# Layer norm of a vision-Mamba kernel: statistics on 64 partitions, the mean subtracted by VectorE, a product on GpSimd

## The chip, the core and the metric

The kernel runs on one core of one Trainium2 chip. The metric is the device time of an execution in microseconds (us). Three runs of the kernel before gave 31715.66, 31737.26 and 31752.72 us; the median is 31737.26 us.

## The reference, cut to what matters

Eight images of 64 x 64 pixels with 96 channels go through four Mamba layers one after the other. Each layer normalizes its input, projects it to 192 inner channels, filters these with a small convolution, runs a selective scan over the pixels (in four directions in layers 0 to 2, in one in layer 3) and comes back to 96 channels. Between the scan and the way back, layers 0 to 2 have a layer norm over the 192 inner channels of each pixel, and then the gate. In layer 0 it reads:

```python
mu = y.mean(-1, keepdims=True)
var = y.var(-1, keepdims=True)
y = (y - mu) * jax.lax.rsqrt(var + 1e-05) * ln_gamma + ln_beta
y = y * jax.nn.silu(z)
return y @ out_proj_w.T
```

Layers 1 and 2 compute the same; layer 3 has the gate and the projection without the norm. All is fp32.

## The kernel before, in words

One hardware loop (L145) runs over the 8 images; its body holds the four layers. Channels lie on partitions and the 4096 pixels of an image along the free axis, in chunks of 512 pixels (CH). The 192 inner channels are more than the 128 partitions, so every inner tensor has two parts: channels 0 to 127 (the tile y_a), and channels 128 to 191, which take 64 partitions (the tile y_b; after the scan its two 64-partition halves each hold a partial sum, which have still to be added).

A layer's scan takes most of its time. The order of its work is written out by hand, slot by slot (the table "plan", L935), and is the same before and after the change. What comes after the scan, from L509 on, is not written out by hand: there the framework decides the order of the instructions on each engine, and each engine then works through its own queue in that order. The framework also sets the semaphores between the engines. One semaphore counter stands for each engine, and a step of it may stand for several instructions.

The stage after the scan has two parts.

*The norm*, L516 to L543, works on a pair of chunks at a time, four pairs a layer. TensorE computes everything that sums over channels, by multiplying with constant matrices:

- "ca" (L524, L525): y_a less its mean, for each of the two chunks. The matrix cen_a is the identity less 1/192, and neg is -1/192 everywhere. A tile of 128 partitions and two banks of PSUM ("wide", two buffers, which the scan uses for "dbu").
- "cb" (L528): y_b less the mean, the two halves of y_b added at the same time. The two chunks stand one above the other in one bank, 64 partitions each ("mm", two buffers).
- The squares of both (L530, L534) are made by ScalarE, and TensorE sums them up to the variance "var" on 128 partitions (L535 from sq_a, L537 from sq_b), in a bank for each chunk (the function "single", the banks y0 and y1, which have one buffer each).
- ScalarE makes 1/sqrt(var + eps) out of it as exp(-0.5 ln(...)) (L540 Ln, L541 Exp). VectorE multiplies ca by it into y_a (L542) and cb into y_b (L543, 64 partitions a chunk).

*The gate stage*, L546 to L596, also works on pairs. GpSimd scales the layer's input (L553, tile "xc", in the pool "decays" with six buffers). TensorE multiplies it by weights (L556 "z_a", one matmul for each chunk in a "wide" tile; L559 "z_b", both chunks in one "mm" bank). ScalarE applies SiLU (L572). VectorE scales the normalized y by gamma and adds beta (L574) and multiplies it by the gate (L582). TensorE projects back to 96 channels (L587, L589, in the banks y0 and y1). VectorE adds the result to the layer's input (L593), takes the statistics for the next layer's normalization (L214), and SyncE writes it to memory (L596). The scan's last additions to y_a and y_b stand in L932, before all this.

A matmul in fp32 shows in the profile as two records. Where a matmul has 64 output columns, two of them, on different columns of the array, can stand side by side.

Of the kernel before, what the change touches and what calls it, by code (L numbers as in the profile page):

```python
# [22 lines left out]
F32 = mybir.dt.float32  # L23
AF = mybir.ActivationFunctionType
ALU = mybir.AluOpType
# [5 lines left out]
DI = 192  # L31
# [4 lines left out]
CH = 512  # L36
# [3 lines left out]


SEL, IDENT, GROUPS, MEAN = 0, 64, 192, 288
NEGMEAN, CEN_A, CEN_B, ONE, EPS, N_CONST = 416, 544, 672, 736, 737, 738


class Layer:
# [61 lines left out]
@contextmanager  # L108
def tables(tc, name):

    load = tc.keep_in_program_order(tc.nc.scalar.preload_act_table_set(name))
    with tc.issue_after(load.ins):
        yield
# [3 lines left out]
def kernel(ctx: ExitStack, tc: tile.TileContext, x_in, const_in, *rest):  # L117
# [27 lines left out]
    with tc.For_i(0, x_in.shape[0], 1) as b:  # L145

        of = x_in[bass.ds(b, 1)].rearrange("o c l -> (o c) l")
        x = load_x(tc, env, of)
        for n, ly in enumerate(LAYERS):
            if n == len(LAYERS) - 1:  # L150
                to = x_out[bass.ds(b, 1)].rearrange("o c l -> (o c) l")
            else:
                to = env.dram.tile([C, L], F32, tag="x", name=f"x_mem{n}")
            x = layer(tc, env, x, of, to, n, ly)
            of = to
# [9 lines left out]
def layer(tc, env, x, x_of, x_to, n, ly):  # L165

    nc = tc.nc
    const, small, big = env.const, env.small, env.big
    sel = const[:, SEL : SEL + 64]
    ident = const[:, IDENT : IDENT + 128]  # L170
    mean_w = const[:, MEAN : MEAN + 128]
    R, K = ly.rank, ly.dirs
    XP = 33 + R

    def mm(name):
        return env.ps_m.tile([128, CH], F32, tag="mm", name=name)

    def wide(name):

        return env.ps_b.tile([128, 2 * CH], F32, tag="dbu", name=name)  # L180
# [4 lines left out]
    def piece(name):  # L185
        return env.deltas.tile([128, CH], F32, tag="delta", name=name)
# [37 lines left out]
    mean = small.tile([C, 1], F32, name="mean")  # L224
# [3 lines left out]
    var = small.tile([C, 1], F32, name="var")  # L228
# [3 lines left out]
    scale = small.tile([C, 1], F32, name="scale")  # L232
# [28 lines left out]
    halves = [slice(0, 64), slice(64, 128)]  # L261
    widths = ((0, 128), (128, 64))

    def single(o, name):
        return env.ps_y.tile([128, CH], F32, tag=f"y{o}", name=name)
# [10 lines left out]
    def u_chunk(half, c):  # L276
        return u0[half][c // 4][0 : widths[half][1], c % 4 * CH : c % 4 * CH + CH]
# [79 lines left out]
    def make_ys():  # L357
        return [big.tile([128, L], F32, tag=f"big{o}", name=f"y{o}") for o in range(2)]

    work = scans(  # L360
        tc, env, n, ly, w, u_mem, lambda half: u_chunk(half, 0), d, neg_a, make_ys, mm, wide
    )
# [145 lines left out]
    y_a, y_b = ys  # L508
# [6 lines left out]
    chunks = [slice(c * CH, (c + 1) * CH) for c in range(NCH)]  # L515
    if ly.norm:  # L516
        with tables(tc, "natural_log_exp_and_others"):
            neg, cen_a = const[:, NEGMEAN : NEGMEAN + 128], const[:, CEN_A : CEN_A + 128]
            cen_b = const[:, CEN_B : CEN_B + 64]
            for c in range(0, NCH, 2):  # L520
                pair = chunks[c : c + 2]
                ca, cb = wide("ca").rearrange("p (o l) -> p o l", o=2), mm("cb")
                for o, s in enumerate(pair):
                    nc.tensor.matmul(ca[:, o], cen_a, y_a[:, s], start=True, stop=False)  # L524
                    nc.tensor.matmul(ca[:, o], neg, y_b[:, s], start=False, stop=True)  # L525
                for first, weights, y in ((True, neg[:, 0:64], y_a), (False, cen_b, y_b)):
                    for s, at in zip(pair, halves):
                        nc.tensor.matmul(cb[at], weights, y[:, s], start=first, stop=not first)  # L528
                sq_b = piece("sq_b")
                nc.scalar.activation(sq_b, cb, AF.Square)  # L530
                var = [single(o, "var") for o in range(2)]
                for o in range(2):
                    sq_a = piece("sq_a")
                    nc.scalar.activation(sq_a, ca[:, o], AF.Square)  # L534
                    nc.tensor.matmul(var[o], mean_w, sq_a, start=True, stop=False)  # L535
                for o, at in enumerate(halves):
                    nc.tensor.matmul(var[o], mean_w[at], sq_b[at], start=False, stop=True)  # L537
                for o, (s, at) in enumerate(zip(pair, halves)):
                    rstd = piece("rstd")
                    nc.scalar.activation(rstd, var[o], AF.Ln, bias=const[:, EPS : EPS + 1])  # L540
                    nc.scalar.activation(rstd, rstd, AF.Exp, scale=-0.5)  # L541
                    nc.vector.tensor_tensor(y_a[:, s], ca[:, o], rstd, ALU.mult)  # L542
                    nc.vector.tensor_tensor(y_b[at, pair[0]], cb[at], rstd[at], ALU.mult)  # L543


    with tables(tc, "silu_and_others"):  # L546
        for c in range(0, NCH, 2):
            pair = chunks[c : c + 2]
            z_a, z_b = wide("z_a").rearrange("p (o l) -> p o l", o=2), mm("z_b")
            xcs = []  # L550
            for o in range(2):
# [3 lines left out]
                at = ly.win_z  # L555
# [29 lines left out]
            at = ly.w_out  # L585
# [8 lines left out]
            if c % 4 == 2:  # L594
                half = slice(c // 4 * L // 2, (c // 4 + 1) * L // 2)
# [445 lines left out]
def constants():  # L1041
    a = np.zeros((128, N_CONST), np.float32)
    for p in range(128):
        a[p, SEL + p % 64] = 1
        a[p, IDENT + p] = 1
    a[32, ONE] = a[96, ONE] = 1
    for p in range(C):
        g = GROUPS + p // GROUP * GROUP
        a[p, g : g + GROUP] = 1 / GROUP
    a[:, MEAN : MEAN + 128] = 1 / DI  # L1050
    a[:, NEGMEAN : NEGMEAN + 128] = -1 / DI
    a[:, CEN_A : CEN_A + 128] = np.eye(128) - 1 / DI
    a[:, CEN_B : CEN_B + 64] = np.tile(np.eye(64), (2, 1)) - 1 / DI
    a[:, EPS] = 1e-5
    return a
# [52 lines left out]
def layouts(inputs):  # L1108
    arrays = {"x": inputs["x"].reshape(-1, L, C).transpose(0, 2, 1), "const": constants()}
    for n, (ly, (pre, names)) in enumerate(zip(LAYERS, _NAMES)):  # L1110
        arrays[f"pack{n}"] = pack(
            ly, inputs[pre + "conv_w"], *(inputs[pre + s] for s in names.split())
        )
    for n, (ly, (pre, _)) in enumerate(zip(LAYERS, _NAMES)):
        arrays[f"conv{n}"] = inputs[pre + "conv_w"].reshape(DI, ly.taps).T.reshape(-1)
    return {f"in_{k}_dram": np.ascontiguousarray(v) for k, v in arrays.items()}
# [20 lines left out]
```

## Time and profile before

| what | value |
|---|---|
| median of the runs | 31737.26 us |
| the profiled execution | 31703.4 us |
| its span on the core | 31698.6 us |
| granted TensorE clock over the span | 0.98 |
| from the last L932 to the first gate (L572), layer 0, image 0 | 38.80 us: TensorE busy 36.32, VectorE 14.75, ScalarE 17.68, GpSimd 3.28, clock 0.99 |
| from there to the end of the layer | 27.42 us: TensorE busy 23.17, VectorE 19.32, ScalarE 7.80, GpSimd 1.17, clock 0.87 |

How to read the lines: a group of instructions has the source line, the engine, the operation, what is written and read, the shape, the count, and behind the bar the busy time in us and the mean of one in ns; behind the second bar stands the engine's idle time before them and what ended it ("<-PE var L537": ScalarE had waited for TensorE's var of line 537). In a timeline the first number is the start in us, the second the duration of the (merged) instructions, and the bracket holds the idle time before. PEld is the loading of weights. In a table of stretches every engine has its busy us and, in brackets, its instructions; the last three figures are the granted clock of TensorE, the DMA share and GB/s. TensorE, VectorE, ScalarE and GpSimd are PE, DVE, ACT and POOL.

### The profile page before, as it was taken

The numbers are of one execution on the slowest core, as the hardware profiler recorded it, in microseconds if no ns is written. First come the engines' busy times: TensorE is split into PE (matmuls) and PEld (weight loads), VectorE is DVE, ScalarE is ACT, GpSimd is POOL, SyncE is SP. The second block draws the span as 40 slices with busy tenths as digits, with TensorE's granted clock in tenths as the row PEclk, the third lists the DMA queues.
The fourth block names the chain that finished last, engine by engine and source line by source line (L and its number), as shares of the span: only waits on it lengthen the run. The fifth ranks groups of instructions, "written<-read, shape, count | busy, mean of one in ns | idle before, by whom it ended". The sixth has DMA issues, their size and how long they took to land. (4 is left out here: it accounts for less than half of the span.)

```text
span 31698.6 us, 951914 instructions
## 1 busy us (share of the span) xinstructions
PE 30814.0 (97%) x402320; PEld 16776.3 (53%) x402320; DVE 28392.2 (90%) x29432; ACT 26085.1 (82%) x65064; POOL 27178.5 (86%) x9436
## 2 busy tenths in 40 slices
PE   9999999999999999999999999999999999999999
PEld 5555555555555545555455554555555555555555
DVE  9899898998989989899898998989989899898998
ACT  8788788887888878888788887878878888788887
POOL 8898788987889879898798987989878898788987
PEclk9999999999999999999999999999999999999999
DMA  3333233333333333333333333333323333333332
GB/s 90 78 76 85 72 90 79 75 86 73 89 80 74 87 72 88 80 74 87 73 88 80 74 87 74 87 79 74 87 72 89 80 74 86 72 90 79 75 86 72
DMA packets 1262156, 2544.89 MB, mean 80 GB/s; under 512 B 108560, under 2 KB 129296, under 8 KB 1234832
## 3 DMA queue, kind: packets, MB, share of 16 engines
q1 hardware_dynamic: 1257872, 2483.64, 33.3%
q8 instruction: 3192, 52.30, 0.7%
q14 instruction: 1092, 8.95, 0.1%
HBM read 2208.74 MB, written 274.46 MB: 78 GB/s over the span
## 5 line engine op out<-in xcount | busy, mean ns | idle before, releaser
L890 POOL TENSOR_TENSOR h<-h,c 128x2048 f32<-128x2048 f32 x4992 | 22723.0, 4557 | 1867.5 <-ACT state L886 625.9
L872 DVE TENSOR_TENSOR_SCAN h<-d_a,state,dbu 128x512 f32<-128x512 f32 x17472 | 21076.5, 1261 | 1130.2 <-PE dbu L841 687.9
L858 ACT ACTIVATE d_a<-delta,neg_a 128x512 f32<-128x512 f32 x19968 | 14166.5, 716 | 122.1 <-DVE h L872 101.3
L841 PE MATMUL dbu<-diag,du_t 64*64 64x128 f32 x319488 | 11142.2, 277 | 296.4 <-DVE h L872 224.7
L841 PEld LDWEIGHTS dbu<-diag,du_t 64*64 64x64 f32 x319488 | 8712.0, 133 | 5111.5 <-issue 4681.5
L904 PE MATMUL y_ps<-h,const 128*64 128x512 f32 x39936 | 10827.0, 617 | 119.1 <-POOL h L890 110.5
L786 ACT ACTIVATE diag<-const,bt 128x64 f32<-128x64 f32 x25600 | 7550.4, 344 | 14.0 <-PE dbu L841 7.8
L773 POOL TENSOR_TENSOR diag<-const,bt 128x512 f32<-128x512 f32 x3328 | 3475.2, 1045 | 335.0 <-ACT bt L747 246.3
L872 DVE TENSOR_TENSOR_SCAN h<-d_a,dbu 128x512 f32<-128x512 f32 x2496 | 2881.8, 1203 | 498.6 <-ACT d_a L858 216.2
L904 PEld LDWEIGHTS y_ps<-h,const 128*64 128x64 f32 x39936 | 2065.6, 135 | 1899.4 <-issue 1498.5
L716 PE MATMUL v<-w,x_dbl 39*128 39x208 f32 (+1 forms) x6656 | 2618.4, 477 | 8.3 <-DVE delta_t L752 7.3
L716 PEld LDWEIGHTS v<-w,x_dbl 39*128 39x128 f32 (+1 forms) x6656 | 1787.2, 317 | 1568.3 <-issue 883.1
L824 ACT COPY delta<-delta_ps 64x512 f32<-64x512 f32 x3328 | 1930.9, 580 | 566.7 <-PE delta_ps L815 519.6
L815 PEld LDWEIGHTS delta_ps<-const,delta_t 128*64 128x64 f32 (+1 forms) x19968 | 1637.0, 154 | 1415.7 <-issue 949.7
L815 PE MATMUL delta_ps<-const,delta_t 128*64 128x128 f32 (+1 forms) x19968 | 2223.8, 286 | 11.6 <-issue 11.6
L747 ACT COPY bt<-v 128x32 f32<-128x32 f32 x1664 | 300.8, 183 | 1848.7 <-PE v L716 1846.5
L730 PEld LDWEIGHTS u_t<-const,u 128*128 128x128 f32 x3328 | 650.1, 195 | 1583.2 <-issue 887.2
L886 ACT COPY state<-h 128x4 f32<-128x4 f32 x4992 | 972.4, 195 | 568.0 <-DVE h L872 527.9
L454 POOL TENSOR_TENSOR acc<-acc,more 128x512 f32<-128x512 f32 x576 | 756.7, 1317 | 699.6 <-ACT more L453 356.1
L730 PE MATMUL u_t<-const,u 128*128 128x128 f32 x3328 | 1292.2, 388 | 0.0
L320 PE MATMUL conv<-xn,taps 96*128 96x512 f32 (+1 forms) x2496 | 1160.0, 658 | 22.1 <-DVE taps L203 22.1
L731 PE MATMUL u_t<-const,u 64*128 64x64 f32 x3328 | 1098.8, 330 | 0.0
(99 smaller groups left out, 16194.5 us busy)
## 6 DMA issues: line engine op xcount, KB each, us to landing
c<-cm SPq DMA_DIRECT2D x1792, 512.0 KB
c<-xm SPq DMA_DIRECT2D x1536, 512.0 KB
u<-u SPq DMA_DIRECT2D x1088, 256.0 KB
u<-u SPq DMA_DIRECT2D x1088, 128.0 KB
u<-u SPq DMA_DIRECT2D x48, 1024.0 KB
x_mem<-x SPq DMA_DIRECT2D x48, 768.0 KB
x<-x_mem SPq DMA_DIRECT2D x48, 768.0 KB
x<-in_x_dram SPq DMA_DIRECT2D x32, 768.0 KB
```

Of the source, the lines that this page charges most:

```text
L320: nc.tensor.matmul(part, taps[:, t, d0 : d0 + nd], rhs, start=t == 0, stop=t == ly.taps - 1)
L716: nc.tensor.matmul(turned[i, e, "v"][:, b], block(2 * e + b, dbls[i]), w[0:XP, at : at + DI + NS], start=True, stop=True,)
L730: nc.tensor.transpose(to[:, b, 0:128], block(b_, u_of(i, 0)), ident)
L773: nc.gpsimd.tensor_tensor(diags[i, 0][:, b], sel.unsqueeze(1).unsqueeze(3).to_broadcast([128, NH, 64, 2]), of.unsqueeze(2).to_broadcast([1 ...
L786: nc.scalar.activation(diags[i, 1][:, b, q // 2, :, q % 2], sel, AF.Copy, scale=turned[i, b // 2, "b"][:, b % 2, NJ + q : NJ + q + 1],)
L815: nc.tensor.matmul(block(b, to), of_, ident, start=True, stop=True)
L824: nc.scalar.copy(delta[64 * half : 64 * half + 64], of)
L841: nc.tensor.matmul(to[64 * half : 64 * half + 64, e, b], du[rows, b, 64 * t : 64 * t + 64], diag[rows, b, 2 * half + pair], start=True, st ...
L858: nc.scalar.activation(d_a, deltas[i, t], AF.Exp, scale=neg_a[:, at : at + 1])
L872: nc.vector.tensor_tensor_scan(hs[s][:, m4, flow], decays.pop(m)[:, flow], p[:, flow], 0.0 if first else states[i // NCH][:, j : j + 1], A ...
L890: nc.gpsimd.tensor_tensor(hs[s], hs[s], cs[i, g], ALU.mult)
L904: nc.tensor.matmul(sums[i][o][64 * half : 64 * half + 64], sel, hs[of][:, state, :], start=g == 0 and e in (0, 4), stop=g == 1 and e in (3 ...
```

## The change

The norm stage is written anew; all else stays.

- The mean of the pair is computed by itself, on 64 partitions a chunk, with the two chunks side by side in one bank ("mean", bank y0). "ca" and its constant cen_a are gone.
- VectorE subtracts the mean from y_a in place. As the mean stands on 64 partitions, it takes two instructions of 64 partitions for each chunk.
- "cb" is computed as before. The square of y_a is taken from SBUF.
- "var" is on 64 partitions a chunk too, both chunks in one bank (bank y1). One Ln serves both. The Exp spreads the result to 128 partitions, with two instructions of 64 partitions for each chunk. The tiles ln and rstd come from the pool "decays" that xc uses, three a pair.
- GpSimd multiplies y_a by it; VectorE multiplies cb into y_b as before.
- The table of constants shrinks from 738 to 482 columns.

```diff
-NEGMEAN, CEN_A, CEN_B, ONE, EPS, N_CONST = 416, 544, 672, 736, 737, 738
+NEGMEAN, CEN_B, ONE, EPS, N_CONST = 352, 416, 480, 481, 482
...
-            neg, cen_a = const[:, NEGMEAN : NEGMEAN + 128], const[:, CEN_A : CEN_A + 128]
-            cen_b = const[:, CEN_B : CEN_B + 64]
+            neg, cen_b = const[:, NEGMEAN : NEGMEAN + 64], const[:, CEN_B : CEN_B + 64]
+            mean_w = const[:, MEAN : MEAN + 64]
             for c in range(0, NCH, 2):
-                pair = chunks[c : c + 2]
-                ca, cb = wide("ca").rearrange("p (o l) -> p o l", o=2), mm("cb")
-                for o, s in enumerate(pair):
-                    nc.tensor.matmul(ca[:, o], cen_a, y_a[:, s], start=True, stop=False)
-                    nc.tensor.matmul(ca[:, o], neg, y_b[:, s], start=False, stop=True)
-                for first, weights, y in ((True, neg[:, 0:64], y_a), (False, cen_b, y_b)):
-                    for s, at in zip(pair, halves):
-                        nc.tensor.matmul(cb[at], weights, y[:, s], start=first, stop=not first)
+                pair = list(zip(chunks[c : c + 2], halves))
+
+                mean, cb = single(0, "mean"), mm("cb")
+                for p, work in (
+                    (mean, ((mean_w, y_a), (mean_w, y_b))),
+                    (cb, ((neg, y_a), (cen_b, y_b))),
+                ):
+                    for last, (weights, y) in enumerate(work):
+                        for s, at in pair:
+                            nc.tensor.matmul(
+                                p[at], weights, y[:, s], start=not last, stop=bool(last)
+                            )
+                var = single(1, "var")
+                for s, at in pair:
+                    for half in halves:
+                        nc.vector.tensor_tensor(
+                            y_a[half, s], y_a[half, s], mean[at], ALU.subtract
+                        )
+                    sq_a = piece("sq_a")
+                    nc.scalar.activation(sq_a, y_a[:, s], AF.Square)
+                    nc.tensor.matmul(var[at], mean_w, sq_a, start=True, stop=False)
                 sq_b = piece("sq_b")
                 nc.scalar.activation(sq_b, cb, AF.Square)
-                var = [single(o, "var") for o in range(2)]
-                for o in range(2):
-                    sq_a = piece("sq_a")
-                    nc.scalar.activation(sq_a, ca[:, o], AF.Square)
-                    nc.tensor.matmul(var[o], mean_w, sq_a, start=True, stop=False)
-                for o, at in enumerate(halves):
-                    nc.tensor.matmul(var[o], mean_w[at], sq_b[at], start=False, stop=True)
-                for o, (s, at) in enumerate(zip(pair, halves)):
-                    rstd = piece("rstd")
-                    nc.scalar.activation(rstd, var[o], AF.Ln, bias=const[:, EPS : EPS + 1])
-                    nc.scalar.activation(rstd, rstd, AF.Exp, scale=-0.5)
-                    nc.vector.tensor_tensor(y_a[:, s], ca[:, o], rstd, ALU.mult)
-                    nc.vector.tensor_tensor(y_b[at, pair[0]], cb[at], rstd[at], ALU.mult)
+                for s, at in pair:
+                    nc.tensor.matmul(var[at], mean_w[at], sq_b[at], start=False, stop=True)
+                ln = env.decays.tile([128, CH], F32, tag="d_a", name="ln")
+                nc.scalar.activation(ln, var, AF.Ln, bias=const[:, EPS : EPS + 1])
+                for s, at in pair:
+                    rstd = env.decays.tile([128, CH], F32, tag="d_a", name="rstd")
+                    for half in halves:
+                        nc.scalar.activation(rstd[half], ln[at], AF.Exp, scale=-0.5)
+                    nc.gpsimd.tensor_tensor(y_a[:, s], y_a[:, s], rstd, ALU.mult)
+                    nc.vector.tensor_tensor(y_b[at, pair[0][0]], cb[at], rstd[at], ALU.mult)
```

The order that the framework gives the changed program: on TensorE, the first of a pair's mean matmuls stands ahead of the previous pair's last var matmuls, the other three behind them. On VectorE, the four subtractions of a pair are mixed with the two y_b products of the pair before (subtraction, product, subtraction, product, subtraction, subtraction), and the three gamma scalings of the pair before follow. On GpSimd, six of the eight products of a layer stand ahead of the first xc, the seventh behind it, then the second xc, the eighth product and the other six xc. In the gate stage z_a and z_b of all pairs stand behind the norm's last matmul; before, the z_a of pair 0 stood ahead of it.

More of the change, by code (lines that the diff above doesn't have):

```diff
@@ L170, in layer @@
     ident = const[:, IDENT : IDENT + 128]
-    mean_w = const[:, MEAN : MEAN + 128]
     R, K = ly.rank, ly.dirs
@@ L1049, in constants @@
         a[p, g : g + GROUP] = 1 / GROUP
-    a[:, MEAN : MEAN + 128] = 1 / DI
-    a[:, NEGMEAN : NEGMEAN + 128] = -1 / DI
-    a[:, CEN_A : CEN_A + 128] = np.eye(128) - 1 / DI
+    a[:, MEAN : MEAN + 64] = 1 / DI
+    a[:, NEGMEAN : NEGMEAN + 64] = -1 / DI
     a[:, CEN_B : CEN_B + 64] = np.tile(np.eye(64), (2, 1)) - 1 / DI
```

## The prediction

> **What bounds the kernel now.** I read the page first, then the groups by line, then the timeline of one layer norm. On the page TensorE (PE) is busy all the time, in every slice.
>
> ```profile
> span 31698.6 us, 951914 instructions
> PE 30814.0 (97%) x402320; PEld 16776.3 (53%) x402320; DVE 28392.2 (90%) x29432; ACT 26085.1 (82%) x65064; POOL 27178.5 (86%) x9436
> ```
>
> A busy share of the whole says little about one stage, so I went to the norm's groups. Three layers with a norm in each of 8 images make 24 norm stages of four pairs of chunks, 96 pairs.
>
> ```profile
> L524 PE MATMUL ca<-y,const 128*128 128x512 f32 x384 | 213.6, 638 | 0.0
> L535 PE MATMUL var<-sq_a,const 128*128 128x512 f32 x384 | 180.5, 592 | 0.0
> L540 ACT ACTIVATE rstd<-var,const 128x512 f32<-128x512 f32 x192 | 130.4, 679 | 297.7 <-PE var L537 297.7
> L542 DVE TENSOR_TENSOR y<-ca,rstd 128x512 f32<-128x512 f32 x192 | 132.8, 691 | 579.7 <-ACT rstd L541 579.7
> L543 DVE TENSOR_TENSOR y<-cb,rstd 64x512 f32<-64x512 f32 x192 | 131.3, 684 | 3.0
> ```
>
> PE waits for nothing there (idle 0.0), ScalarE (ACT) waits for PE, VectorE (DVE) for ACT: PE sets the pace. The timeline of the stage that begins at 1138 us gives the period of a pair:
>
> ```profile
> 1150.85 1.12 PE L524 MATMUL ca<-y,const 128*128 128x512 f32 x2
> 1152.77 1.94 PE L528 MATMUL cb<-y,const 128*64 128x512 f32 x8
> 1154.63 1.12 PE L524 MATMUL ca<-y,const 128*128 128x512 f32 x2
> 1156.45 1.88 PE L535 MATMUL var<-sq_a,const 128*128 128x512 f32 x4
> 1158.27 1.13 PE L537 MATMUL var<-sq_b,const 64*128 64x512 f32 x4
> 1159.32 1.12 PE L524 MATMUL ca<-y,const 128*128 128x512 f32 x2
> ...
> 1177.52 1.52 POOL L553 TENSOR_SCALAR xc<-x,scale,shift 96x512 f32<-96x512 f32 x2 [34.29 <-PE z_b L559]
> 1178.36 0.67 DVE L543 TENSOR_TENSOR y<-cb,rstd 64x512 f32<-64x512 f32 x1
> 1178.99 0.69 DVE L542 TENSOR_TENSOR y<-ca,rstd 128x512 f32<-128x512 f32 x1
> 1179.71 0.69 DVE L543 TENSOR_TENSOR y<-cb,rstd 64x512 f32<-64x512 f32 x1
> 1179.83 3.75 PE L556 MATMUL z_a<-xc,w 96*128 96x512 f32 x4 [2.48 <-DVE y L542]
> ```
>
> From start to start: 1.92 (ca of one chunk) + 1.86 (cb, four matmuls in two columns of the array) + 1.82 (ca) + 1.82 (var) + 1.05 (var from sq_b) = 8.47 us. At the end PE stands still for 2.48 us, and the same two matmuls then take 3.75 us instead of 2. The stretches show why:
>
> ```profile
> 1180.00:1182.00 2.00, 2.00 (x3) 0.97 (x4) 1.97 (x4) 1.83 (x4) 0.00 (x0) 0.50 0.00 0
> 1188.00:1190.00 2.00, 2.00 (x7) 0.57 (x4) 2.00 (x4) 0.60 (x1) 0.00 (x0) 1.00 0.00 0
> ```
>
> The granted clock (third figure from the end) was 0.50 after the gap and 1.00 later.
>
> **What the Trainium skill says.** "TensorE: Matmul & The Clock Gate", Part 1: an idle window of some 3.4 us halves the clock until a busy one has passed. The trace agrees and is stricter: a 2.48 us gap was enough here. "TensorEngine Tiling (Array Packing)", Key Properties: tiles work side by side, a change of tiling mode drains the array. The trace agrees: eight cb records took 1.94 us, as four of var did (1.88). "VectorE: DVE Perf Modes", Two Vector instructions with no wait between them: an instruction whose inputs or output start in another quadrant of partitions is held until the one before has finished. The trace agrees: from L543 on the low half to L542 it is 0.63 us from start to start, from L542 to L543 on the upper half 0.72. "GPSIMD Engine Reference", 3.1: an addition of two fp32 tensors of 2048 takes 4497 ns; L890 shows 4557. The same page, 8, says that GpSimd blocks VectorE only where the latter has two SBUF inputs or a two-port mode; the new subtractions have one input in PSUM, so I add nothing. No run here shows it for this pair of operations.
>
> **The change part by part.** Times t count from the end of the last addition to y_b (1141.47 in the stage above). Durations: an fp32 matmul is two passes 0.43 apart, 0.86, its result 0.16 later; DVE 0.69; Square 0.60, Ln 0.69, Exp 0.63, starting 0.52 apart (two L534 took 1.08 in all, so neighbours overlap by 0.11); a hand-over between engines 0.05. GpSimd's (POOL's) product of 128x512: 1.14 (a quarter of L890) to 1.32 (L454's mean), and I take 1.32.
>
> *PE's work.* Four mean and four cb matmuls run two by two, 4 x 0.86; var twice 0.86; var from sq_b 0.86 and some 0.2 for two changes of mode. That is 5.4 to 6.2 us in place of 8.47. If PE stayed the bound, up to 3 us a pair, 290 us in all, would be won.
>
> *The new chain.* It does not stay the bound. "mean" has a single bank (y0), which the next pair gets when this pair's last subtraction is done; and the order of the changed program's instructions on each engine says what follows. Count from the end of that subtraction. Square of the second half: 0.69 with its hand-overs. var from it: 0.86. var from sq_b, with a change of mode: 0.95. Only behind that stand the next pair's other three mean matmuls: 0.91 and 1.02 to the end of the last, for which the first subtraction waits (the semaphore is raised there), 0.05. The subtractions are priced by L543, the nearest row (same height, one input in PSUM): 0.67 to 0.70. DVE then has six instructions in a row, two of them the y_b products of the pair before: 0.65 + 4 x 0.72 + 0.69 = 4.2, since nearly each changes its quadrant. Sum 8.7, against 8.47. The four Exp, POOL's two products (2.64) and the three scalings by gamma (1.5) fit beside it: they cost nothing while POOL stays below some 4 us a pair.
>
> *First and last pair.* The first is quicker: its matmuls need neither ca nor a second round, and its Ln starts at t = 7.6 instead of 9.48. Three more periods: 7.6 + 3 x 8.7 = 33.6 against 34.9, so 1.3 earlier.
>
> *Hand-over to the gate stage.* Before, all xc (L553) but two stood in front: POOL was idle for 34.29 us, and z_a and z_b of pair 0 were done inside the norm. Now POOL's queue has the xc of the second chunk behind the last pair's first product, which needs rstd at 35.4: 35.5 + 1.32 + 0.77 = 37.6. Then z_a until 38.6, and the first gate, whose semaphore comes after both z_a, starts at 38.7 (before: 38.8). The 1.3 are gone. And PE, which bounds the gate stage (before: at work from 38.3 to 60.3 but for one gap of 1.4), has half of z_a and the z_b of pair 0 in it as well, 2 us: it begins 0.7 earlier and has 2.0 more to do, with some 0.3 of waiting for gates behind gamma scalings that wait for POOL. +1.6 us a stage, 38 us in all.
>
> *The clock.* In 17 of 24 stages the clock fell at the 2.48 us gap; stages without it ended 63.2 after the start, the mean of all is 65.4, so about 1.8 a stage go to the clock (layer 1's undisturbed 64.2 counted). Now there are gaps of 1.9 (pair 0 to 1), 1.0 (the next two) and 3.1 us (before z_a). Bounds: zero more, if only the last gap counts and as before; 2.7, if the 1.9 us gap halves the clock in most stages and the last one keeps it down longer. Estimate: 1.7. It stretches the matmul part of the chain and PE's gate stage.
>
> *Other edits.* A smaller constant table: one transfer at the start. Nothing else moves: outside this stage the engines' orders are the same, and SyncE's too.
>
> Sum: 1.6 + 1.7 = 3.3 a stage, x 24 = 79 us. The profiled execution took 31703.4 (span 31698.6), so 31782; the median of the runs is 34 higher, so 31816.
>
> **The rivals.** (1) *The clock costs nothing more*: a gap of 1.9 is too short and the last counts as before. For it: several gaps of 1.4 passed without a drop. Against: 3.1 is longer than 2.48. Then 38 us: 31775, not slower than the 0.2% (63 us) that a measurement of this kernel can tell from no change. This decides between "same" and "slower": the point is 1.0 us of clock a stage. (2) *PE's relief comes through*: VectorE does not hold the half-height instructions and the first subtraction gets its half early. The chain is then 7.6, the gate stage starts 2.6 earlier, less the 2 us of z: with an unthrottled clock (-1.8) a stage wins 2.8, 31670. Against: the 0.72 in the trace, and the semaphore's place in the program. (3) *The clock stays down through the norm*: each pair's 4.4 us of matmul chain is stretched by half, 2.2 x 3 pairs more, 24 stages: +160, 31975. Against: between gaps PE is busy for 7 us on end.
>
> **How the numbers follow.** Forecast 0.55, rival 1 0.28, rival 2 0.07, rival 3 0.10. Slower 0.65, same 0.28, faster 0.07. The range goes from below rival 1 (DVE or POOL quicker by 2 us a stage, 31725) to halfway to rival 3, 31900.
>
> **What would show it.** Right: first Ln near 7.6 after the last y addition, Ln every 8.7; the first subtraction (L535) released by PE mean, PE's mean by DVE; first z_a idle 3 us on POOL xc; gates of pair 0 not earlier; stage end later by 1.5 to 4 with stretches at 0.50 inside the norm. Wrong: Ln 7.7 apart, DVE half-height instructions 0.62 apart, clock at 1.00 throughout, or a span changed outside these stages.

## The result, and the profile after

The changed kernel took 31850.72 us (median of 6 runs, 31832.14 to 31876.31), the kernel before 31740.61 in the same comparison (6 runs). The ratio is 1.0036, with a 95% interval of 1.0023 to 1.0049: slower by 110 us, and inside the predicted range. The forecast was 31816. The two terms of its sum were both wrong, though, in opposite directions, so that part of the nearness is luck; that took experiments to see.

The page of the kernel after, its span and the busy times of the engines:

```profile
span 31827.0 us, 952418 instructions
PE 30757.8 (97%) x402320; PEld 16682.2 (52%) x402320; DVE 28604.9 (90%) x29624; ACT 26165.5 (82%) x65160; POOL 27458.9 (86%) x9628
```

TensorE is 97% busy as before and GpSimd has 280 us more; nothing here says where 128 us of span went. The groups of the norm say more (line, shapes, count | busy us, mean ns | idle time before them and what ended it):

```profile
L535 DVE TENSOR_TENSOR y<-y,mean 64x512 f32<-64x512 f32 x384 | 263.3, 686 | 318.3 <-PE mean L529 279.9 <-PE cb L529 32.4
L551 POOL TENSOR_TENSOR y<-y,rstd 128x512 f32<-128x512 f32 x192 | 243.6, 1269 | 742.8 <-ACT rstd L550 600.8 <-DVE y L552 140.4
L540 PE MATMUL var<-sq_a,const 128*64 128x512 f32 x384 | 208.2, 624 | 123.1 <-ACT sq_a L539 120.0
L565 PE MATMUL z_a<-xc,w 96*128 96x512 f32 x512 | 313.9, 714 | 76.6 <-POOL xc L562 76.6
L583 DVE TENSOR_SCALAR y<-y,w 128x512 f32<-128x512 f32 x288 | 202.2, 750 | 34.9 <-POOL y L551 31.7
```

TensorE now waits inside the norm (L540, idle 123.1 us, for ScalarE's squares), VectorE waits for the mean (L535), and z_a waits for GpSimd's xc: 76.6 us in all, 3.2 a stage. The last line holds something that the prediction did not have: the scaling by gamma takes 750 ns on average. In the kernel before the same work had

```profile
L574 DVE TENSOR_SCALAR y<-y,w 128x512 f32<-128x512 f32 x288 | 142.2, 543 | 3.2
```

One period of the loop, in the timeline of the changed kernel's first stage (its last addition to y ends at 1141.64):

```profile
1149.38 0.69 ACT L546 ACTIVATE ln<-var,const 128x512 f32<-128x512 f32 x1 [1.76 <-PE var L544]
1151.17 0.68 DVE L535 TENSOR_TENSOR y<-y,mean 64x512 f32<-64x512 f32 x1 [4.70 <-PE mean L529]
1153.86 1.07 PE L540 MATMUL var<-sq_a,const 128*64 128x512 f32 x2 [1.87 <-ACT sq_a L539]
1158.14 0.69 ACT L546 ACTIVATE ln<-var,const 128x512 f32<-128x512 f32 x1 [1.70 <-PE var L544]
```

The first Ln starts 7.74 after the addition, and the next 8.76 later; the further two periods are 8.88 and 8.84. Then the hand-over to the gate stage, in the same timeline:

```profile
1177.94 1.27 POOL L551 TENSOR_TENSOR y<-y,rstd 128x512 f32<-128x512 f32 x1 [5.53 <-DVE y L552]
1179.18 0.77 POOL L562 TENSOR_SCALAR xc<-x,scale,shift 96x512 f32<-96x512 f32 x1
1179.24 2.22 DVE L583 TENSOR_SCALAR y<-y,w 128x512 f32<-128x512 f32 x1 [1.32 <-POOL y L551]
1180.00 2.07 PE L565 MATMUL z_a<-xc,w 96*128 96x512 f32 x2 [3.20 <-POOL xc L562]
1182.11 1.09 ACT L581 ACTIVATE gate<-z_a 128x512 f32<-128x512 f32 x2 [1.67 <-PE z_a L565]
1185.78 3.62 PE L596 MATMUL out<-gate,w 128*96 128x512 f32 x4
```

GpSimd makes the last pair's first product, then the second xc, and only then can TensorE go on, after 3.20 us of standing still. Its matmuls then take about twice as long (2.07 for what takes 1.12 at full clock), and the stretch behind the wait shows the granted clock (third figure from the end) at 0.50:

```profile
1180.00:1182.00 2.00, 2.00 (x2) 0.50 (x2) 1.97 (x2) 0.45 (x1) 2.00 (x2) 0.50 0.00 0
```

The gamma scaling beside the xc and the second product takes 2.22 us in place of 0.54.

For all 24 stages of the one profiled execution of each kernel I took four times from the trace, in us and as means. The first three are counted from the end of the last addition to y: the start of the last Ln, the start of the first gate, and the end of the stage (the start of the one instruction on VectorE, L220 before and L219 after, that draws the next layer's statistics together). The fourth is how long the granted clock was at a half within the stage.

| kernel | last Ln | first gate | stage end | at half clock | ratio to before, 95% interval |
|---|---|---|---|---|---|
| before | 36.48 | 39.13 | 65.36 | 4.34 | 1 |
| after | 34.42 | 40.48 | 69.86 | 9.81 | 1.0036 [1.0023, 1.0049] |
| e1_fill | 34.36 | 39.68 | 68.13 | 2.22 | 1.0027 [1.0017, 1.0037] |
| e2_wide | 29.81 | 35.95 | 65.36 | 11.14 | 1.0004 [0.9996, 1.0012] |
| e3_dve | 40.71 | 45.31 | 71.88 | 9.24 | 1.0047 [1.0033, 1.0061] |
| e4_var64 | 32.70 | 37.31 | 62.21 | 3.28 | 0.9986 [0.9980, 0.9993] |
| e5_last | 34.60 | 39.20 | 67.01 | 5.28 | 1.0012 [1.0005, 1.0018] |
| e6_wide_last | 29.78 | 34.38 | 61.58 | 4.31 | 0.9971 [0.9960, 0.9981] |
| e7_wide_fill | 29.73 | 35.11 | 62.87 | 2.33 | 0.9982 [0.9974, 0.9989] |
| e8_wlf | 29.80 | 34.41 | 63.13 | 4.41 | 0.9993 [0.9985, 1.0001] |
| e9_full | 40.43 | 45.04 | 73.59 | 8.48 | 1.0068 [1.0055, 1.0082] |
| e10_fill1 | 29.90 | 34.51 | 61.87 | 3.54 | 0.9974 [0.9964, 0.9985] |

The changed kernel's stages end 4.50 us later: 24 x 4.50 = 108 us of the 128 by which the spans differ. The other 20 lie outside these stages. The time there, 30130 us before, was between 30124 and 30183 in all these kernels, so I explain nothing with it. The experiments are read by this table as much as by the total times, since the intervals of the ratios reach 20 to 45 us to each side. The ends of one kernel's 24 stages scatter by 0.6 to 1.2 us (standard deviation), so a mean of them is good to some 0.2.

### The profile page after: what moved, and what is told of

Same layout as the page of the kernel before. It is cut to its first block, busy times and chain, and to the rows that moved or that the text cites. A ratio compares the mean times of both kernels' runs of the same rounds, so it can differ in the third digit from the quotient of the medians.

```text
span 31827.0 us, 952418 instructions
## 1 busy us (share of the span) xinstructions
PE 30757.8 (97%) x402320; PEld 16682.2 (52%) x402320; DVE 28604.9 (90%) x29624; ACT 26165.5 (82%) x65160; POOL 27458.9 (86%) x9628
## 5 line engine op out<-in xcount | busy, mean ns | idle before, releaser
L725 PE MATMUL v<-w,x_dbl 39*128 39x208 f32 (+1 forms) x6656 | 2614.0, 476 | 12.0 <-DVE delta_t L761 11.1
```

The source lines that it names most:

```text
L725: nc.tensor.matmul(turned[i, e, "v"][:, b], block(2 * e + b, dbls[i]), w[0:XP, at : at + DI + NS], start=True, stop=True,)
```

## The experiments

My first reading was that the clock costs more than predicted: 9.81 - 4.34 = 5.5 us more at half clock, half of it lost, 2.7 a stage against the 1.7 forecast. That would leave 1.8 for the rest, near the forecast 1.6. The rival was that the clock goes along and the structure of the stage costs more. The first four runs shared a chip; their expectations are written for the times above, and on that chip the kernel before had a median of 31707.6, so that the ratios have to be compared.

**e1_fill: keep TensorE at work in the gap.**

```diff
-                nc.tensor.matmul(z_a[:, o], w[0:C, at : at + 128], xc, start=True, stop=True)
+                for _ in range(4 if ly.norm and c == 0 and o == 0 else 1):
+                    nc.tensor.matmul(z_a[:, o], w[0:C, at : at + 128], xc, start=True, stop=True)
```

> The changed kernel, with the first z_a matmul of pair 0 issued four times in place of once (the same product written four times), so that PE has work in the 3.2 us in which it waits for the last xc. Theory (the granted clock is halved by that gap, and PE sets the end of the gate stage): most of the 9.8 us that PE now spends at half clock in each of the 24 stages go, half of that is lost time, less what the clock costs elsewhere; a stage ends 1.5 to 4 us earlier, so 31755 to 31815 against 31851. Rival (the end is set by the late xc and by the longer list of work behind it, the clock only goes along): the same time as the changed kernel within 15 us, though the clock in the records is up.

Time at half clock fell from 9.81 to 2.22 us a stage, and the stage ended only 1.73 earlier. By the stages that is the low end of what the theory gave; by the total the ratio went from 1.0036 to 1.0027, with overlapping intervals, which leaves both theories open. What decides is that ten of its 24 stages ran with (almost) no half clock at all, less than 0.6 us, which no stage of the changed kernel did: they ended at 67.23 (layers 0 and 2) and 66.87 (layer 1). The kernel before had four such stages: 63.23 (layer 2; layer 0 had the same first gate) and 64.20 (layer 1). So without any throttle the changed structure is later by 4.00 and 2.67, on average (16 and 8 stages) 3.56 us a stage. The added matmuls lie in a wait and delay nothing there: 0.6 us of the wait is left (the first line below), and the order on every engine is otherwise that of the changed kernel.

Where the 4.00 lies is seen in a stage of layer 2 at full clock. In this kernel (last y addition at 7525.36):

```profile
7563.73 1.12 PE L566 MATMUL z_a<-xc,w 96*128 96x512 f32 x2 [0.64 <-POOL xc L562]
7564.90 1.09 ACT L582 ACTIVATE gate<-z_a 128x512 f32<-128x512 f32 x2 [0.73 <-PE z_a L566]
7568.43 1.96 PE L597 MATMUL out<-gate,w 128*96 128x512 f32 x4 [1.42 <-DVE gate L592]
```

and in the kernel before (last y addition at 3542.16):

```profile
3580.52 1.96 PE L556 MATMUL z_a<-xc,w 96*128 96x512 f32 x4 [2.48 <-DVE y L542]
3580.96 1.09 ACT L572 ACTIVATE gate<-z_a 128x512 f32<-128x512 f32 x2
3582.34 1.96 PE L587 MATMUL out<-gate,w 128*96 128x512 f32 x4
```

Both start this stretch of z_a at the same time, 38.37 and 38.36. Before, it is pair 1's z_a and the out matmuls follow at 40.18. Now it is the second half of pair 0's z_a, its z_b and half of pair 1's z_a, and then TensorE waits 1.42 us for the first gate product: out starts at 43.07, 2.89 later. Another 1.11 comes after that, where the other half of pair 1's z_a is made; the other waits of TensorE are the same to 0.1 us.

**e2_wide: give the mean two buffers.** The tile is free in the norm once ca is gone.

```diff
-                mean, cb = single(0, "mean"), mm("cb")
+                mean, cb = wide("mean")[:, 0:CH], mm("cb")
```

> The changed kernel, with the mean in a PSUM tile that has two buffers instead of in the one bank y0. Theory (the bank, given back only at the last subtraction, closes the loop of 8.8 us from one Ln to the next): the next pair's mean matmuls run ahead, the Ln come 6 to 7.8 us apart, the last Ln of a stage comes 3 to 8 us earlier, and the stage ends 2 to 5 us earlier: 31730 to 31800. Rival (the six half-height instructions on VectorE, or PE at half clock, set the 8.8 us): the Ln stay 8.4 to 8.8 apart and the time stays within 20 us of the changed kernel's 31851.

The four Ln in its first stage:

```profile
1149.96 0.69 ACT L546 ACTIVATE ln<-var,const 128x512 f32<-128x512 f32 x1 [2.61 <-PE var L544]
...
1156.46 0.69 ACT L546 ACTIVATE ln<-var,const 128x512 f32<-128x512 f32 x1 [1.69 <-PE var L544]
...
1164.47 0.67 ACT L546 ACTIVATE ln<-var,const 128x512 f32<-128x512 f32 x1
...
1170.64 0.69 ACT L546 ACTIVATE ln<-var,const 128x512 f32<-128x512 f32 x1 [1.75 <-PE var L544]
```

They are 6.5, 8.0 and 6.2 apart instead of 8.8, and the last comes 4.6 us earlier than in the changed kernel: it was the single bank that closed the loop, and the rival (six half-height instructions on VectorE, or TensorE at half clock, set the pace) falls. With the second buffer the framework also put the instructions on three engines into another order; the run shows the effect of both together. The stage ends 4.50 earlier, level with the kernel before, with 11.1 us of it at half clock.

**e3_dve: one part undone, the product back on VectorE.**

```diff
-                    nc.gpsimd.tensor_tensor(y_a[:, s], y_a[:, s], rstd, ALU.mult)
+                    nc.vector.tensor_tensor(y_a[:, s], y_a[:, s], rstd, ALU.mult)
```

> The changed kernel, with one part undone: the product of the first 128 channels with rstd is back on VectorE. Theory (the product on GpSimd holds the last xc back, and both engines slow each other there): the two last products no longer stand ahead of xc in GpSimd's queue, the first xc waits only for its place in the list, z_a starts 1.5 to 2.5 us earlier and the gamma scalings take 0.54 again; but VectorE gets 1.4 us more work a pair, in the loop from Ln to Ln: 8.8 becomes 9.3 to 10.2. Sum: 31830 to 31900, about the changed kernel's time. Rival (GpSimd's product hides behind other work and costs nothing where it is): the Ln come later and nothing is won at the end, 31890 to 31960.

Both halves of this came true, the second more than the first. From the last Ln to the first gate it takes 4.6 us in place of 6.1, from there to the end 26.6 in place of 29.4, and the gamma scalings are nearly back:

```profile
L583 DVE TENSOR_SCALAR y<-y,w 128x512 f32<-128x512 f32 x288 | 153.3, 575 | 4.0
```

But the Ln are 11.0 apart and the last comes 6.3 us later, where I had at most 4.2. So GpSimd's product is worth it in the loop, and costs at the hand-over. By its ratio the run lies where the ranges of both theories meet; the stages show that both are at work.

**e4_var64: one part of the change alone, on the kernel before.** The variance on 64 partitions side by side, one Ln, four Exp; ca and the products as before. Two things differ from that part as it stands in the change: the bank of "var" alternates from pair to pair, and the tiles ln and rstd come from another pool (the function piece).

```diff
-                var = [single(o, "var") for o in range(2)]
-                for o in range(2):
+                var = single(c // 2 % 2, "var")
+                for o, at in enumerate(halves):
...
-                    nc.tensor.matmul(var[o], mean_w, sq_a, start=True, stop=False)
-                for o, at in enumerate(halves):
-                    nc.tensor.matmul(var[o], mean_w[at], sq_b[at], start=False, stop=True)
+                    nc.tensor.matmul(var[at], mean_w[:, 0:64], sq_a, start=True, stop=False)
+                for at in halves:
+                    nc.tensor.matmul(var[at], mean_w[at, 0:64], sq_b[at], start=False, stop=True)
+                ln = piece("ln")
+                nc.scalar.activation(ln, var, AF.Ln, bias=const[:, EPS : EPS + 1])
...
-                    nc.scalar.activation(rstd, var[o], AF.Ln, bias=const[:, EPS : EPS + 1])
-                    nc.scalar.activation(rstd, rstd, AF.Exp, scale=-0.5)
+                    for half in halves:
+                        nc.scalar.activation(rstd[half], ln[at], AF.Exp, scale=-0.5)
```

> The kernel before, with one part of the change alone: the variance of two chunks on 64 partitions side by side, one Ln for both and four Exp; centring and products as before. Theory (PE sets the pace of the kernel before, 8.47 us a pair): PE's work for var falls by some 0.9 us a pair, the Ln come 7.5 us apart, the stage ends 1.5 to 4 us earlier: 31640 to 31705 against 31741. Rival (the two Exp more and the single Ln move the loop to ScalarE or to the wait for both variances, and the gate stage starts no earlier because of the first products): 31725 to 31780.

The Ln come 7.9 apart, the last one 3.8 us earlier than before, and the stage ends 3.15 earlier: faster, 0.9986. So this part of the change, done in this way, is a gain; what made the whole slower lies in the rest of it, or in how the parts go together.

**e5_last: only the last pair's product on VectorE.** The hand-over without the loop.

```diff
-                    nc.gpsimd.tensor_tensor(y_a[:, s], y_a[:, s], rstd, ALU.mult)
+                    mult = nc.vector if c == NCH - 2 else nc.gpsimd
+                    mult.tensor_tensor(y_a[:, s], y_a[:, s], rstd, ALU.mult)
```

> The changed kernel, with the product with rstd of the last pair of each stage alone back on VectorE; the other three pairs keep theirs on GpSimd. Theory (the structure that costs the time is the hand-over: GpSimd has the last product and then xc in one queue, and its product holds up the gamma scaling on VectorE): the Ln stay 8.8 apart, the last Ln at 34.4; from the last Ln to the first gate 4.6 us in place of 6.1, from there to the end of the stage 26 to 27.5 in place of 29.4; the stage ends near 65.5, 4.3 earlier, so 100 us less than the changed kernel: 1.0000 to 1.0012 times the kernel before. Rival (the longer rest of work on TensorE behind the first gate is what counts, wherever the product is): the gate comes 1.5 us earlier and the end at most 1.5 earlier, 1.0024 or more.

```profile
1176.98 1.09 ACT L582 ACTIVATE gate<-z_a 128x512 f32<-128x512 f32 x2
...
1178.73 3.16 PE L597 MATMUL out<-gate,w 128*96 128x512 f32 x4 [2.49 <-DVE gate L592]
```

The first gate no longer waits for TensorE, and comes 4.6 us after the last Ln as expected. z_a and z_b of pair 0 are done inside the norm again, so TensorE's list behind the first gate is short again. The stage ends 2.85 us earlier than in the changed kernel, more than the rival allows (1.5) and less than the theory wanted (4.3): TensorE, early now, waits 2.49 us for the first gate product, and the clock falls there in its turn.

**e6_wide_last: both remedies** (the edits of e2_wide and e5_last).

> Mean in the tile with two buffers, and the last pair's product on VectorE: both remedies at once. Theory (the bank of the mean and the hand-over are two costs in series): the last Ln near 29.8, the first gate 4.6 later at 34.4, the stage ends 26 to 27.5 after that, at 60.5 to 62, that is 3.4 to 4.9 us before the kernel before: 0.9963 to 0.9974 times its time. Rival (what is won early is lost again at half clock or in a list of work on TensorE that cannot start earlier): the stage ends at 63 or later, 0.9982 or more.

As the theory had it: last Ln 29.8, gate 34.4, end 61.6. The ratio is 0.9971 [0.9960, 0.9981], so this version beats both kernels, by 0.3% and by 0.65%.

**e7_wide_fill: e2_wide, with the first z_a of pair 0 four times** (the edit of e1_fill).

> Mean in the tile with two buffers, and the first z_a matmul of pair 0 issued four times to fill the 3.2 us before xc. Theory: the clock is worth what filling was worth with the one bank, 1.7 us a stage, or a little more since 11.1 us a stage are at half clock: the stage ends at 63 to 63.8 in place of 65.4, 0.9981 to 0.9988 times the kernel before. Rival (the clock falls in gaps elsewhere too, at the third pair's Ln, and the fill comes too late): 65 and no change, 1.0000 to 1.0006.

The end came 2.49 earlier than in e2_wide and half clock fell from 11.14 to 2.33. With e1_fill that makes two measurements of what the gap before xc does by way of the clock: 1.7 and 2.5 us a stage, for 7.6 and 8.8 us at half clock. Only about a quarter of that time is lost, not half. That TensorE is not on the path all the time in the gate stage is my reading of it; no run tests it.

**e8_wlf and e10_fill1: fill the wait before the first out matmul, in e6_wide_last.** The same edit with four z_a in pair 1 (c == 2, o == 0), and with three in pair 0 (c == 0, o == 1).

> Mean in the tile with two buffers, the last pair's product on VectorE, and the first z_a matmul of pair 1 (the last work that TensorE has before it waits for the first gates) issued four times, the same product each time. Theory (what is left of half clock in the stage, 4.3 us, comes from this wait of 1.6 to 2.5 us and is worth half of it): time at half clock falls below 1.5 us a stage, the stage ends near 60 in place of 61.6, 0.9957 to 0.9963 times the kernel before. Rival (the repeated matmuls stand in front of the out matmuls and take back what the clock gives): the stage ends at 61.2 or later, 0.9968 or more.

> As the run before the last (mean in the tile with two buffers, last pair's product on VectorE), with the second z_a matmul of pair 0 issued three times, which by the order of the program's instructions stands where it is wanted, ahead of the wait for the first gates; the attempt with the repeats on pair 1 had put three of them behind the first out matmuls. Theory (a gap of 2.5 us before the first out costs the clock 3.4 us at half speed, so 1.7 a stage): the gap is 0.8, half clock falls below 2 us a stage, the stage ends between 59.9 and 60.8 in place of 61.6, 0.9958 to 0.9966 times the kernel before. Rival (what is at half clock after that gap is not what sets the end): 61.4 or later, 0.9969 or more.

Neither gave anything. In e8_wlf the framework put the three repeats behind the first out matmuls, where they hide nothing, and changed the order behind them: the gap of 2.5 us stayed and the stage ends 1.55 later. In e10_fill1 the matmuls stood where they were wanted, but gaps of 1.6 us were left. Here they are in its first stage, which happened to stay at full clock, with another gap in the norm:

```profile
1169.56 1.07 PE L540 MATMUL var<-sq_a,const 128*64 128x512 f32 x2 [2.19 <-ACT sq_a L539]
...
1178.94 1.96 PE L598 MATMUL out<-gate,w 128*96 128x512 f32 x4 [1.60 <-DVE gate L593]
```

Half clock only fell from 4.31 to 3.54, and the end is 61.87 against 61.58, within the scatter: the expectation failed, and the rival's range came true. The trace does not bear out the rival's reason, though. Within e10_fill1 the seven stages whose only drop came behind the wait for the gates ended at 62.2 to 62.3, and the three that had none before their last microsecond at 60.6: such a drop does cost 1.6. Two things took the gain back. In 14 stages (12 in e6_wide_last) the half clock began at 27 to 28.6, 2.2 to 3.7 us after the start of the gap of 2.19, which the edit does not touch. And the framework changed VectorE's order with the edit: the second gamma scaling, 0.92 us beside GpSimd, now stands ahead of the first gate product, so that at full clock the first out starts at 36.46 in place of 35.63. By as much, stages with a drop in the same place end later than in e6_wide_last (62.2 to 62.3 against 61.4 to 61.5). So this run does not measure the fill alone.

**e9_full: the mean on full height, in e6_wide_last.** The mean stands on 128 partitions; its constant matrix (mean_f) has 128 columns.

```diff
-                mean, cb = wide("mean")[:, 0:CH], mm("cb")
-                for p, work in (
-                    (mean, ((mean_w, y_a), (mean_w, y_b))),
...
+                mean, cb = wide("mean").rearrange("p (o l) -> p o l", o=2), mm("cb")
+                for o, (s, at) in enumerate(pair):
+                    for last, y in enumerate((y_a, y_b)):
+                        nc.tensor.matmul(
+                            mean[:, o], mean_f, y[:, s], start=not last, stop=bool(last)
...
-                    for half in halves:
-                        nc.vector.tensor_tensor(
-                            y_a[half, s], y_a[half, s], mean[at], ALU.subtract
+                    nc.vector.tensor_tensor(y_a[:, s], y_a[:, s], mean[:, o], ALU.subtract)
```

> Mean in the tile with two buffers and the last pair's product on VectorE, with one size changed: each chunk's mean on all 128 partitions in a half of its own, so that VectorE subtracts in two instructions of full height a pair instead of four of half height, and TensorE makes four mean matmuls of full width, one after the other, instead of two by two. Theory (with the bank free, TensorE is again the closer bound): 1.7 us more of matmul a pair, the Ln 7.5 to 8 apart in place of 7.1, the last Ln near 31.5 in place of 29.8, the stage ends 1 to 2 us later than with half height: 0.9978 to 0.9987 times the kernel before. Rival (the half-height instructions on VectorE, 0.70 each, set the pace): the Ln come 6 to 6.8 apart, the last Ln before 29.3, the stage ends at 61.2 or earlier, 0.9967 or less.

The direction is the theory's, the size is not (1 to 2 us were expected): the Ln are 10.6 apart on average and the stage ends 12 us later. In the timeline of its first stage:

```profile
1154.68 1.94 PE L530 MATMUL cb<-y,const 128*64 128x512 f32 x8
...
1155.48 1.53 DVE L582 TENSOR_SCALAR y<-y,w 128x512 f32<-128x512 f32 x1 [1.33 <-POOL y L550]
...
1157.04 0.69 DVE L551 TENSOR_TENSOR y<-cb,rstd 64x512 f32<-64x512 f32 x1
1157.77 1.28 DVE L535 TENSOR_TENSOR y<-y,mean 128x512 f32<-128x512 f32 x2
...
1162.95 0.69 ACT L544 ACTIVATE ln<-var,const 128x512 f32<-128x512 f32 x1 [2.75 <-PE var L542]
```

The mean matmuls, longer now, push cb further behind the previous pair's Ln. But cb is done at 1156.62, and the subtractions start 1.15 later without a wait of their own, when VectorE has finished what now stands ahead of them in its queue: the products of the pair before, and a gamma scaling that waited 1.33 us for GpSimd's product and then took 1.53 beside GpSimd. It is so in all 24 stages: ahead of the first subtraction of the second, third and fourth pair stands a gamma scaling of 1.5 us, and cb has been done for 1.1 to 1.4 us. So the experiment did not change one size alone, as the framework put the instructions into a new order with it, and it does not answer its question. I did not take apart how much of the 12 us each wait costs.

## Why the prediction was right, and where it was not

The forecast was "slower", at 31816, by 3.3 us a stage; measured are 31851 and 4.5. The mechanism of the loop and the wait at the hand-over were forecast rightly. That the sum came near is in part luck: the hand-over was put 2.0 us a stage too low and the clock 0.8 too high. Step by step:

- *The loop.* 8.7 us forecast, 8.76 to 8.88 measured; first Ln 7.6 against 7.74. The single bank of "mean" was named as what closes the loop, and e2_wide shows it. The forecast that VectorE holds half-height instructions is also seen: 0.69 to 0.72 from start to start.
- *TensorE's work of a pair*, forecast at 5.4 to 6.2 where it was 8.47: over one period of 8.88 us (1158.14 to 1167.02) TensorE shows 7.87 us busy. Part of the difference is that matmuls that stand alone take 1.07, as shown, not the 0.86 of a row of them. It did not matter, as the loop is not TensorE's. The records of 1.94 and 1.88 us named in the forecast show that the array's tiles work side by side; what a change of mode costs no run shows by itself.
- *Hand-over.* The forecast named the right queue and the right wait (z_a for xc behind the last product). Its times: the product at 35.5, z_a at 37.6, the gate at 38.7; measured 36.3, 38.4 and, without throttle, 39.5. Of this delay 0.6 is the last Ln (34.2 against 33.6: the first Ln came 0.14 later, and the three periods were longer by 0.4 in all). Most of the rest is the two Exp that the first product needs: they were taken to start 0.52 apart because two Square overlap by 0.11, but Exp on 64 partitions took 2.57 for four, 0.64 each, without overlap.
- *What the hand-over costs: the step that failed*, +1.6 a stage. It was made of "begins 0.7 earlier", "2.0 more to do" and "some 0.3 of waiting". Measured without throttle in layers 0 and 2: TensorE begins no earlier (38.37 against 38.36), has 2.6 more to do (4.0 less the new wait) and waits 1.4 before the first out. Together 4.0, and 3.56 with layer 1.
- *The clock*, +1.7 a stage. The mean without throttle is 67.11 (from e1_fill) and the changed kernel's is 69.86, so the clock takes 2.75; before it took 65.36 - 63.55 = 1.81. The change added 0.94, not 1.7. The gaps of the first stage were as forecast (1.87, 1.01, 1.03 and 3.20 us, with one of 1.08 besides). My first reading after the result was wrong: the drop is in all 24 stages and over twice as long, but it costs only 0.94 more, not the 2.7 that half of the added time would be. 3.56 + 0.94 = 4.5, the measured sum. This takes e1_fill's stages at full clock for those of the changed kernel, which has none of its own.
- *The rivals.* The clock was nearly rival 1 (1.0 a stage was its point of decision), but its 31775 took the 1.6 for granted. TensorE's relief (rival 2) did not come through with the single bank. In rival 3's place, the half clock inside the norm, only 5 of 24 stages had 3.4 us of it, at about t = 32.
- *Contention, judged only in part.* I wrote that the subtractions, with one input in PSUM, are not blocked by GpSimd: they are not (0.686 on average). I did not look at what else stands beside GpSimd's product, the gamma scaling. The Trainium skill has it in "SBUF — State Buffer", Who interferes with whom: a tensor_scalar of VectorE can run in a two-port mode, and then contends with GpSimd for a pair of ports; whichever starts first has the pair for its whole instruction, and the other is blocked. The trace agrees in that the scaling takes 0.54 alone and up to 2.23 beside GpSimd, while the mean went from 543 to 750 ns and back to 575 with the product on VectorE. In the stage of e1_fill shown above VectorE and GpSimd did this ahead of the first out (7568.43):

```profile
7562.96 2.23 DVE L584 TENSOR_SCALAR y<-y,w 128x512 f32<-128x512 f32 x1 [1.32 <-POOL y L551]
7563.64 1.27 POOL L551 TENSOR_TENSOR y<-y,rstd 128x512 f32<-128x512 f32 x1
7565.23 0.69 DVE L552 TENSOR_TENSOR y<-cb,rstd 64x512 f32<-64x512 f32 x1
7565.95 1.83 DVE L584 TENSOR_SCALAR y<-y,w 128x512 f32<-128x512 f32 x2
7567.70 2.29 DVE L592 TENSOR_TENSOR gate<-gate,y 128x512 f32<-128x512 f32 x3
```

The three scalings took 4.06 us, where three at 0.54 take 1.62. An estimate from these lines: with scalings of 0.54 the second would start when GpSimd's second product is done (7564.91), and the gates some 1.8 us earlier than they did, which is more than the wait of 1.42 before the first out. No run tests it, so how much of the wait is due to contention is open; e5_last has no product on GpSimd there and waits 2.49, though from an earlier start.

## What to carry to other kernels

When a change replaces a wait, ask which buffer closes the new loop: here one bank with a single buffer held it at 8.8 us, and another, already idle tile brought the last Ln 4.6 us forward. A product moved to a less busy engine should be followed to the end of the loop: there it stands ahead of the next stage's first work in the queue, and doing the last one elsewhere won 2.85 us a stage. And a longer time at half clock is not a loss in proportion; find a stage without it, or make one, before dividing by two. Last, where a framework orders the instructions, look at the new order before an experiment is read: in e9_full and e10_fill1 a gamma scaling had moved ahead of the very work that was to come earlier.

## What was not expected of the hardware

- In each trace all drops of the granted clock but one lasted 3.41 us or a multiple of it (6.83, 10.24, 13.65 and longer). Which gaps bring it down is not fixed by their length alone: 1.42 us was followed by a drop in some stages of e1_fill, 2 us after the gap began, and by none in others with the same gaps.
- One drop of 3.41 us costs 1.6 to 1.7 us where TensorE sets the end (68.87 against 67.23 in layers 0 and 2 of e1_fill, 68.55 against 66.87 in layer 1).
- A product of 128x512 in fp32 on GpSimd took 1.27 us, a gamma scaling caught beside it up to 2.23.
